# The last layernorm of a four-stage transformer kernel, taken apart: batches normed before the last pair of experts, and that pair's rows summed and written by slot

## The chip, the cores and the metric

The kernel runs on one core of a Trainium2 chip. The metric is the device time of one execution in microseconds (us); lower is better. Five runs of the kernel before give a median of 963.58 us (958.40 to 966.50). The trace that all readings come from is of one more execution, which took 962.57 us; 960.8 us of it lie between the first and the last instruction (the span), at a mean granted TensorE clock of 0.971.

Names: PE is TensorE (PEld its weight loads), DVE is VectorE, ACT is ScalarE, POOL is GpSimd, SP is SyncE, which here only issues DMAs. All data are fp32.

## The reference

The input is x of shape 8 x 512 x 256 (batches, positions, channels). Two layers follow each other, each of an attention part and a feed-forward part, and after each of the four parts `x = layernorm(x + part(x))`. The fourth part is a mixture of experts, and it is the one that the change touches:

```
x = input_emb.reshape(G=2, T=2048, H=256)            # two groups of 4 batches
gate, idx = top_k(softmax(x @ w_router), 2)          # 8 experts, two for each token
# every expert of a group takes at most C=160 slots; later tokens are dropped
expert_in  = einsum('gtec,gth->egch', dispatch, x)
h          = relu(expert_in @ wi[e])                 # 256 -> 1024
expert_out = h @ wo[e]                               # 1024 -> 256
y          = einsum('gtec,egch->gth', combine, expert_out)   # gate * row, added to the token
out        = layernorm(x + y)                        # no scale, no bias
```

A token can be in two experts, in one, or (if both were full) in none.

## The kernel before

**Routing and slots.** The experts are handled in pairs. A pair has 320 slots (160 for each expert), held as three columns of 128, 128 and 64 slots (`COLS`), so that a group has 4 pairs and 12 columns (`NJ`). `route(g)` makes two tables of shape 128 x 12 for a group: `srcs[g]`, the token that sits in each slot, and `gates[g]`, its gate. A slot that stayed empty gets the number of one of 128 spare rows behind the group's 2048 tokens, and gate 0.

**Buffers in HBM.** `x3_d[g]` holds the normed rows of a group, from which the experts read, and `y_d[g]` holds the same rows again as the sum into which the experts' rows are added.

**One expert.** `load_expert` loads `wi` and `wo` (1 MB each) on SP's queue; `EW = 3` experts fit at a time. `gather` fetches the rows of a pair by `srcs` (three indirect DMAs of POOL), `dispatch` transposes them on PE (tile `xs_tp`), `expert_in` is the first matmul (`wi_ps`, with the ReLU on ACT into `e_hT`), `expert_out` the second (`wo_ps`, copied by DVE into `eoT`). `combine` transposes a column back (`eo_tp`) when all its slots are done, scales it by the gates on ACT (`eo`), and adds its rows into `y_d[g]` by an indirect DMA of POOL with `compute_op=add`. Each of these scatter-adds to one `y_d` waits until the one before has landed.

Group 0 goes through experts 0 to 7, group 1 through 7 to 0, so that three experts' weights serve both groups in turn. Step i is the i-th of these 16 (tiles carry this number: `wi_13` is the weights of step 13). The last pair of group 1 is experts 1 and 0, steps 14 and 15.

**The end.** `finish(g)` begins for a group when its last `combine` has ended (key `("s", (g + 1) * E - 1)`): for each batch it loads z, 512 rows of `y_d[g]`, norms it (`layernorm`: statistics on DVE, the power -0.5 on POOL into `ln_rs`, then the scaling, for group 0 on DVE and for group 1 on ACT with a bias `ln_nb` from DVE), and stores it to `out`. For group 0 the four batches follow one another while group 1's experts run; for group 1 all four are loaded at once.

**What sets the order.** Every engine's queue is in fixed order, and that order is planned ahead of time: `interleave` holds a list of streams of stages (keys such as `("h", i)` expert_in, `("e", i)` expert_out, `("s", i)` combine, `("f", g)` finish, `("w", i)` weights, `("r", g)` route), and keeps a model of when engines, PSUM banks and buffers come free (`Plan`, `op`, `pe`, `need`), with costs written out by hand. It always emits the work that the model says can start first. A stage waits for the keys that it names and for free buffers of the tags that it takes. `op` is the helper that emits all planned work of ACT, DVE, POOL and SP, so most of their rows in the profile carry one line, L205; the tile names tell them apart. Where the model sees PE idle for over 1.4 us it puts in `spare` matmuls.

The semaphores' waits come on top of this: an instruction whose data is late holds up all that is queued behind it on its engine.

Of the kernel before, what the change touches and what calls it, by code (L numbers as in the profile page):

```python
# [11 lines left out]
F32 = mybir.dt.float32  # L12
F32R = mybir.dt.float32r
I32 = mybir.dt.int32
# [6 lines left out]
P = 128  # L21
# [6 lines left out]
E = 8  # L28
# [53 lines left out]
def tile_layers(ctx: ExitStack, tc: tile.TileContext, ins, out, at):  # L82
# [41 lines left out]
    def rows_of(d, b):  # L124
        g, r = divmod(b * S, TG)
        return d[g][r : r + S, :].rearrange("(c p) d -> p c d", p=P)
# [39 lines left out]
    def give(tag, t, n=1):  # L166
        Plan.free[tag] += [t] * n
# [67 lines left out]
    def release(ps, t):  # L235
        Plan.banks[Plan.bank_of.pop(id(ps))[1]] = t
# [15 lines left out]
    def later(t):  # L252

        return "other", t

    def interleave(streams):
# [11 lines left out]
        first = {"a1", "b", "c1", "h", "e", "s", "d"}  # L268
# [182 lines left out]
    def route(g, pool):  # L451
# [99 lines left out]
        def sources():  # L551
            nc.vector.tensor_scalar(emp, src, 0.0, float(TG), ALU.is_equal, ALU.mult)
            nc.vector.tensor_scalar(row0, src, 0.0, tokid[:, 0:1], ALU.is_equal, ALU.mult)
            nc.vector.tensor_tensor(emp, emp, row0, ALU.add)
            nc.vector.scalar_tensor_tensor(srcs[g], src, -1.0, emp, ALU.add, ALU.add)
# [9 lines left out]
    with ExitStack() as stages:  # L565
# [15 lines left out]
        def dma(t, out, in_):  # L581
            op(SP, 0.0, t, nc.sync.dma_start, out=out, in_=in_)
# [947 lines left out]

        def combine(i):

            g, e = order[i]
            pair, half = divmod(e, 2)
# [3 lines left out]
            for j, n in enumerate(COLS):  # L1538
# [14 lines left out]
                )  # L1553
                done = op(
# [10 lines left out]
            return done + 2.9  # L1565

        def finish(g):
            for b in range(g * B // G, (g + 1) * B // G):
                z = wk.tile([P, NC, D], F32, tag="x", bufs=XB, name=f"z_{b}")
                t = Plan.t  # L1570
                dma(t, z, rows_of(y_d, b))
                landing = t + (9.0 if g == 0 else 4.0)
                e = max(layernorm(wk, z, z, [landing] * NC, on_act=(g == 1))[3])
                dma(e, out[b].rearrange("(c p) d -> p c d", p=P), z)
                if g == 0:
                    yield later(e + 4.0)
            give("x", e + 4.0, 1 if g == 0 else XB)
            yield later(e + 4.0)
            return e + 4.0

        def after(*keys):
# [62 lines left out]
            ],  # L1644
            [
                (("f", g), [("s", (g + 1) * E - 1)], {"x": 1 if g == 0 else XB}, finish(g))
                for g in range(G)
# [32 lines left out]
```

## Time and profile before

| | |
|---|---|
| median of 5 runs | 963.58 us (958.40 to 966.50) |
| profiled execution | 962.57 us, span 960.8 us |
| busy in the span | PE 894.9 us (93%), DVE 609.2 (63%), ACT 445.4 (46%), POOL 394.5 (41%) |
| last expert matmul (`wo_ps`) | starts 924.30 us, the run of 32 takes 4.51 us |
| last three scatter-adds into `y_d` | issued 925.79, 930.62, 935.13 us |
| loads of group 1's four batches (`z<-y_d`) | issued from 938.73 us on |
| stores of them (`out<-z`) | issued from 948.63 us on, each lands 2.8 us later |

Times within the execution count from the start of the span. A row of the timeline gives start, duration, engine, line, operation, `out<-in` by the program's names (without numbers), shapes, and how long the engine stood idle before it and what ended that. The time of a DMA instruction is that of its issue; it lands later. "Clock" is the share of full speed that the throttle granted TensorE, in the table by stretches of time its mean. "issue" as a releaser means that the profile shows nothing that the engine waited for.

### The profile page before, as it was taken

The numbers are of one execution on the slowest core, as the hardware profiler recorded it, in microseconds if no ns is written. First come the engines' busy times: TensorE is split into PE (matmuls) and PEld (weight loads), VectorE is DVE, ScalarE is ACT, GpSimd is POOL, SyncE is SP. The second block draws the span as 40 slices with busy tenths as digits, with TensorE's granted clock in tenths as the row PEclk, the third lists the DMA queues.
The fourth block names the chain that finished last, engine by engine and source line by source line (L and its number), as shares of the span: only waits on it lengthen the run. The fifth ranks groups of instructions, "written<-read, shape, count | busy, mean of one in ns | idle before, by whom it ended". The sixth has DMA issues, their size and how long they took to land.

```text
span 960.8 us, 18726 instructions
## 1 busy us (share of the span) xinstructions
PE 894.9 (93%) x7676; PEld 702.3 (73%) x7676; DVE 609.2 (63%) x1485; ACT 445.4 (46%) x862; POOL 394.5 (41%) x395
## 2 busy tenths in 40 slices
PE   7999999999999998999999899979999999999960
PEld 4777777777777786778667666657686898999860
DVE  2855446788668678667889788857765853512213
ACT  2237266356834943581656155632655534122213
POOL 3246446432554543372436224362365223253331
PEclk9999999999999999899999899989999999999995
DMA  6030000002000100200020000001503357349735
GB/s 214 2 110 2 2 1 2 2 1 67 1 2 23 45 1 1 67 1 2 1 68 1 1 32 15 2 1 45 190 15 107 130 169 213 67 121 332 215 64 180
DMA packets 49653, 60.36 MB, mean 63 GB/s; under 512 B 5536, under 2 KB 44960, under 8 KB 49568
## 3 DMA queue, kind: packets, MB, share of 16 engines
q1 hardware_dynamic: 45600, 53.92, 16.9%
q0 software_dynamic: 3968, 5.25, 3.2%
q8 instruction: 60, 0.98, 0.4%
q14 instruction: 25, 0.20, 0.1%
HBM read 43.43 MB, written 15.73 MB: 62 GB/s over the span
## 4 chain that ended last, share of the span: by engine, by line
PE 66%; DVE 19%; ACT 6%; POOL 4%; issue 3%; DMA 2%; POOLq 0%; SPq 0%; ACTq 0%; DVEq 0%
PE wi_ps L1484 7%; PE wo_ps L1513 7%; PE pr_ps L1121 6%; PE qk_ps L1201 4%; PE fc_ps L1092 4%; PE qk_ps L876 4%; PE hs L1260 3%; PE w_ps L1354 3%; PE r_ps L957 3%; PE tp L348 3%; PE at_ps L1275 2%; DVE a L205 2%; PE w_ps L1343 2%; PE sc L924 2%; PE v_ps L1207 2%
## 5 line engine op out<-in xcount | busy, mean ns | idle before, releaser
L1121 PE MATMUL pr_ps<-prT,fT 128*128 128x257 f32 x512 | 117.1, 382 | 0.3 <-ACT scm L205 0.3
L1121 PEld LDWEIGHTS pr_ps<-prT,fT 128*128 128x128 f32 x512 | 95.5, 189 | 16.6 <-issue 1.9
L205 POOL TENSOR_TENSOR fsq<-fsq,fsf 128x512 f32<-128x512 f32 x56 | 72.6, 1296 | 30.6 <-ACT fsf L205 28.1
L1484 PE MATMUL wi_ps<-xsT,wi 128*128 128x160 f32 x512 | 77.2, 305 | 0.0
L205 ACT ACTIVATE e_hT<-wi_ps 128x480 f32<-128x480 f32 (+1 forms) x48 | 25.3, 527 | 105.7 <-PE wi_ps L1484 105.7
L1513 PE MATMUL wo_ps<-e_hT,wo 128*128 128x160 f32 x512 | 73.5, 300 | 0.0
L1484 PEld LDWEIGHTS wi_ps<-xsT,wi 128*128 128x128 f32 x512 | 72.5, 194 | 0.7 <-issue 0.2
L1513 PEld LDWEIGHTS wo_ps<-e_hT,wo 128*128 128x128 f32 x512 | 70.5, 190 | 1.0 <-issue 0.6
L205 DVE TENSOR_TENSOR hm<-hs,cst 128x512 f32<-128x512 f32 x96 | 60.0, 676 | 15.5 <-PE hs L1260 15.5
L205 POOL DMA_INDIRECT y_d<-eo,srci x24 | 37.2, 1550 | 77.3 <-ACT eo L205 40.2
L205 POOL TENSOR_TENSOR ln_rs<-ln_rs,mhalf 128x4 f32<-128x4 f32 x32 | 34.1, 1065 | 84.2 <-DVE ln_rs L205 84.2
L205 POOL TENSOR_TENSOR scm<-scm,cst 128x512 f32<-128x512 f32 x32 | 43.8, 1367 | 55.0 <-ACT scm L205 55.0
L205 DVE TENSOR_TENSOR scm<-sc,cst 128x512 f32<-128x512 f32 x96 | 60.1, 677 | 8.9 <-PE sc L924 8.8
L1201 PE MATMUL qk_ps<-l1T,x2T 128*128 128x512 f32 x128 | 61.7, 603 | 0.0
L205 POOL TENSOR_TENSOR hm<-hm,cst 128x512 f32<-128x512 f32 x32 | 40.9, 1280 | 48.2 <-ACT hm L205 48.2
L205 DVE STREAM_TRANSPOSE hT<-pad 128x512 f32<-128x512 f32 x64 | 59.3, 959 | 2.1 <-ACT pad L205 1.4
L876 PE MATMUL qk_ps<-xT,wqkv 128*128 128x512 f32 x128 | 60.2, 613 | 0.2 <-DMA wqkv<-in_L_attn_W_qkv 0.2
L1092 PE MATMUL fc_ps<-x1T_l,fcT 128*128 128x512 f32 x128 | 53.7, 419 | 2.8 <-DVE x1T_l L205 1.5
L1092 PE MATMUL fc_ps<-x1T_h,fcT 128*128 128x512 f32 x128 | 50.8, 397 | 0.0
L205 ACT ACTIVATE x<-x,ln_nb,ln_rs 128x256 f32<-128x256 f32 x64 | 33.2, 590 | 31.2 <-DVE ln_nb L205 31.2
L205 DVE COPY eoT<-wo_ps 128x320 f32<-128x320 f32 x16 | 7.8, 489 | 59.2 <-PE wo_ps L1513 59.2
L205 ACT ACT_TABLE_LOAD x33 | 42.3, 1283 | 1.3 <-PEq L1666 0.7
(240 smaller groups left out, 1997.3 us busy)
## 6 DMA issues: line engine op xcount, KB each, us to landing
wi<-in_L_ffn_wi SPq DMA_DIRECT2D x13, 1024.0 KB, 6.0
wo<-in_L_ffn_wo SPq DMA_DIRECT2D x13, 1024.0 KB, 6.2
x<-in_L_attn_x SPq DMA_DIRECT2D x8, 512.0 KB, 3.9
x_d<-a SPq DMA_DIRECT2D x8, 512.0 KB, 3.0
y_d<-a SPq DMA_DIRECT2D x8, 512.0 KB, 4.1
z<-y_d SPq DMA_DIRECT2D x8, 512.0 KB, 5.1
out<-z SPq DMA_DIRECT2D x8, 512.0 KB, 3.0
prepare<-in_L_ffn_W_fc SPq DMA_DIRECT2D x1, 1024.0 KB, 10.6
```

Source lines behind the costliest of these rows:

```text
L205: heapq.heappush(Plan.events, (t, Plan.count, lambda: fn(*args, **kw)))
L348: T.transpose(ps[:, c * P : (c + 1) * P], src[:, c, k * P : (k + 1) * P], ident)
L876: T.matmul(ps, wqkv[:, k, which * D + m * P : which * D + (m + 1) * P], xT[:, k, :], start=(k == 0), stop=(k == NK - 1),)
L924: T.matmul(sc[p][:, m * 256 : (m + 1) * 256], kT[rows, m, cs], qz[c][rows, m, :, :], start=True, stop=True,)
L957: T.matmul(acc[32 * p : 32 * p + 32, m * P : (m + 1) * P], vz[c][:, m * 4 + p, 32 * j : 32 * j + 32], scm[p][:, m * 2 + j, :], start=False ...
L1092: T.matmul(ps, fcT[:, k, f * P : (f + 1) * P], x[:, k, :], start=(k == 0 and x is low), stop=(k == NK - 1 and x is high),)
L1121: T.matmul(acc[:, : D + 1], hT[:, f, c * P : (c + 1) * P], prT[:, f, :], start=(f == 0), stop=(f == NF - 1),)
L1201: T.matmul(qk, x2T[:, k, cs], l1T[:, k, 0:2, :].rearrange("p a d -> p (a d)"), start=(k == 0), stop=(k == NK - 1),)
L1260: T.matmul(sc[r][:, g * P : (g + 1) * P], hT[rows, g, P : 2 * P], hT[rows, g, :P], start=True, stop=True,)
L1354: T.matmul(acc[:, :D], hT[:, k, c * P : (c + 1) * P], l1T[:, k, 4, :], start=(k == 0), stop=(k == NK - 1),)
L1484: T.matmul(ps[:, f * CAP : (f + 1) * CAP], wi[:, k, (f3 + f) * P : (f3 + f + 1) * P], x[:, k, es], start=(k == 0), stop=(k == NK - 1),)
L1513: T.matmul(ps[:, m * CAP : (m + 1) * CAP], wo[:, f, m * P : (m + 1) * P], hT[:, f, :], start=(f == 0), stop=(f == NF - 1),)
```

## The change

1. Group 1's batches are loaded, normed and stored by a `finish(b)` of their own each, from the end of `combine` of step 13 on: with all experts in them but the last pair (1 and 0).
2. That pair's columns (0, 1, 2) are no longer added into `y_d`. Their scaled rows `eo` stay in SBUF. `meet`, right after the routing, builds `tail_same`: for each of the 320 slots, which of the 320 hold the same token (1.0 or 0.0), from the token numbers spread over all partitions by three matmuls with the identity, and three compares on DVE. `fetch` gathers the 320 slots' rows of `y_d` (as they are after step 13). `sums` multiplies `tail_same` with the rows, so that each slot has the sum of both experts' rows for its token: nine matmuls of 256 columns in three PSUM banks. `finish_last` adds this to the fetched rows, norms them slot by slot, and writes them to their rows of `out` by three indirect DMAs, which wait for all plain stores. Two slots with one token write the same bytes.
3. An empty slot of the last pair now has a token's number (its own partition, 0 to 127) instead of a spare row; with gate 0 it takes part in that token's sum with zeros and writes that token's row.
4. Group 0's batches are finished in two streams side by side ((0, 1) and (2, 3)) instead of one.

The plan is made anew with this. In the planned queues nothing changes place up to the end of group 1's routing. From group 1's second pair on, PE has some `wi_ps` groups ahead of transposes that they followed before; SP has the loads of z_0 and z_2 together, then both stores and the loads of z_1 and z_3 together; the stores of z_1 and z_3 stand ahead of the weights of steps 14 and 15.

```diff
-        first = {"a1", "b", "c1", "h", "e", "s", "d"}
+        first = {"a1", "b", "c1", "h", "e", "s", "d", "z"}
...
             nc.vector.tensor_scalar(row0, src, 0.0, tokid[:, 0:1], ALU.is_equal, ALU.mult)
+            if g == G - 1:
+                nc.vector.memset(emp[:, :3], 0.0)
             nc.vector.tensor_tensor(emp, emp, row0, ALU.add)
...
+        tail, stored = {}, []
         def combine(i):
             g, e = order[i]
+            last = i >= len(order) - 2
...
                     scale=gates[g][:n, col : col + 1], bank=ps, use="scm",
                 )
+                if last:
+                    tail[j], done = eo, t
+                    continue
                 done = op(
                     POOLD, 1.87, max(t, Plan.landed), GP.indirect_dma_start,
                     out=y_d[g], in_=eo[:n], in_offset=None, compute_op=ALU.add,
...
-            return done + 2.9
-        def finish(g):
-            for b in range(g * B // G, (g + 1) * B // G):
-                z = wk.tile([P, NC, D], F32, tag="x", bufs=XB, name=f"z_{b}")
-                t = Plan.t
-                dma(t, z, rows_of(y_d, b))
-                landing = t + (9.0 if g == 0 else 4.0)
-                e = max(layernorm(wk, z, z, [landing] * NC, on_act=(g == 1))[3])
-                dma(e, out[b].rearrange("(c p) d -> p c d", p=P), z)
-                if g == 0:
-                    yield later(e + 4.0)
-            give("x", e + 4.0, 1 if g == 0 else XB)
+            return done + (0.0 if last else 2.9)
+        def meet():
+            g = G - 1
+            token = pools[0].tile([P, 3], F32, tag="tail_token", name="tail_token")
+            row = pools[0].tile([P, 3], I32, tag="tail_row", name="tail_row")
+            def rows():
+                nc.vector.tensor_copy(token, srcs[g][:, :3])
+                nc.vector.tensor_scalar(row, srcs[g][:, :3], g * TG, None, ALU.add)
...
+            for j, n in enumerate(COLS):
+                T.matmul(
+                    ps[:, j * P : j * P + n], token[:, j : j + 1].to_broadcast([P, P]),
+                    ident[:, :n], start=True, stop=True,
+                )
+            same = wk.tile([P, 3, 2 * CAP], F32, tag="T", bufs=TB, name="tail_same")
+            t = pe(0.7)
+            for j in range(3):
+                e = op(
+                    DVE, 0.52, t, V.tensor_scalar,
+                    same[:, j, :], ps[:, : 2 * CAP], token[:, j : j + 1], None, ALU.is_equal,
+                )
...
+        def fetch():
...
+            for j, n in enumerate(COLS):
+                t = op(
+                    POOLD, 1.3, t, GP.indirect_dma_start,
+                    out=y[:n, j, :], out_offset=None, in_=y_d[g],
+                    in_offset=bass.IndirectOffsetOnAxis(ap=srcs[g][:n, j : j + 1], axis=0),
+                )
...
+        def sums(ks, end):
...
+            for j, n in enumerate(COLS):
+                for k in ks:
+                    nk = COLS[k]
+                    T.matmul(
+                        tail["ps"][j][:n, :D], same[:nk, k, j * P : j * P + n], tail[k][:nk],
+                        start=(first and k == ks[0]), stop=(end and k == ks[-1]),
+                    )
...
+        def finish_last():
+            y, (_, row) = tail["y"], tail["same"]
...
+            for j, n in enumerate(COLS):
+                z = y[:n, j, :]
...
+                def stats(z=z, st=st, mv=mv, n=n):
+                    nc.vector.bn_stats(st[:n], z)
+                    nc.vector.bn_aggr(mv[:n], st[:n])
+                    nc.vector.tensor_scalar(st[:n, :1], mv[:n, 1:2], 1.0, LN_EPS, ALU.mult, ALU.add)
+                def put(z=z, j=j, n=n):
+                    nc.gpsimd.memset(between, 0.0)
+                    w = nc.gpsimd.indirect_dma_start(
+                        out=rows, in_=z, in_offset=None,
+                        out_offset=bass.IndirectOffsetOnAxis(ap=row[:n, j : j + 1], axis=0),
+                    )
+                    for store in stored:
+                        tc.add_manual_dep(w.ins, store.ins.name, ...)
+                    for other in written:
+                        tc.declare_no_dep(w.ins, other.ins, reason="the same bytes")
+                    written.append(w)
+                ps = tail["ps"][j]
+                t = op(DVE, 0.45, Plan.t, V.tensor_tensor, z, z, ps[:n, :D], ALU.add, bank=ps)
+                t = op(DVS, 0.8, t, stats)
+                t = op(
+                    POOL, 0.56, t, GP.tensor_tensor, st[:n, :1], st[:n, :1], mhalf[:n], ALU.pow
+                )
+                t = op(
+                    DVS, 0.41, t, V.tensor_scalar,
+                    z, z, mv[:n, 0:1], st[:n, 0:1], ALU.subtract, ALU.mult,
+                )
+                t = op(POOLD, 1.6, max(t, tail["stored"]), put)
...
+        def finish(b):
+            g = b * G // B
+            z = wk.tile([P, NC, D], F32, tag="x", bufs=XB, name=f"z_{b}")
+            t = Plan.t
+            dma(t, z, rows_of(y_d, b))
+            landing = t + (9.0 if g == 0 else 4.0 + 2.9 * (b - B // G))
+            yield later(landing)
+            e = max(layernorm(wk, z, z, [landing] * NC, on_act=(g == 1))[3])
+            def store():
+                stored.append(
+                    nc.sync.dma_start(out=out[b].rearrange("(c p) d -> p c d", p=P), in_=z)
+                )
+            op(SP, 0.0, e, store)
...
+            [(("z", 2), [("z", 1), ("y", 0)], {}, finish_last())],
+            *(
+                [
+                    (("f", b), [("s", (1 + b // half) * E - (1, 3)[b // half])], {"x": 1}, finish(b))
+                    for b in bs
+                ]
+                for bs in ([0, 1], [2, 3], [4], [5], [6], [7])
+            ),
             [
-                (("f", g), [("s", (g + 1) * E - 1)], {"x": 1 if g == 0 else XB}, finish(g))
-                for g in range(G)
+                (("m", 0), [("r", G - 1)], {"T": 1}, meet()),
+                (("y", 0), [("s", n - 3)], {"T": 1}, fetch()),
+                (("z", 0), [("s", n - 2)], {}, sums((2,), False)),
+                (("z", 1), [("s", n - 1)], {}, sums((0, 1), True)),
             ],
```

## Prediction

> **What bounds the kernel now.** I read the page first, then the chain of waits from 880 us on, then windows for clock and DMA, and last POOL's own order.
>
> ```profile
> span 960.8 us, 18726 instructions
> PE 66%; DVE 19%; ACT 6%; POOL 4%; issue 3%; DMA 2%; POOLq 0%; SPq 0%; ACTq 0%; DVEq 0%
> ```
> PE carries the path except at the very end. The chain, cut to the pieces used below (start, duration, what):
>
> ```profile
> 888.53 1.43 POOL y_d L205
> 889.96 1.09 POOL ln_rs L205
> 891.08 1.38 DVE z L205 x4
> 892.46 0.41 DVE eoT L205
> 892.92 0.66 PE eo_tp L1546 x4
> ...
> 924.46 4.36 PE wo_ps L1513 x32
> 928.85 0.50 DVE eoT L205
> ...
> 930.62 3.78 DMA y_d<-eo,srci
> 934.44 0.69 issue
> 935.13 3.58 DMA y_d<-eo,srci
> 938.73 3.92 DMA z<-y_d
> ...
> 954.58 0.60 ACT z L205
> ```
> Two things show. The last expert matmul ends at W = 924.46 + 4.36 = 928.8; after it lie 32.0 us without expert work: two scatter-adds in a row, load of four batches, their layernorm, stores. And at 891 the chain leaves PE: a scatter-add on POOL, the power of one batch's norm queued behind it, the norm on DVE, and behind the norm the copy `eoT` that PE's transposes need. PE stood still from 891.04 to 892.92, 1.9 us. What the stall did to the clock, from the table by stretches (us; PE, PEld, DVE, ACT, POOL busy; granted clock; DMA share; GB/s):
>
> ```profile
> 891.00:894.48 3.48, 1.76 (x12) 1.11 (x10) 1.78 (x5) 1.66 (x4) 0.36 (x2) 1.00 1.02 312
> 894.48:897.89 3.41, 3.41 (x14) 3.40 (x14) 0.00 (x0) 0.93 (x3) 1.28 (x1) 0.50 1.08 343
> ```
> Clock 0.50 for 3.41 us costs another 1.7, so the stall costs 3.6 in all. Why was POOL late? The scatter-add issued at 873.24 landed 8.0 us later, and the next one, to the same rows, waited for it. The DMA queues from 873.3 to 877.3, then from 877.3 to 881.3:
>
> ```profile
> q1 hardware_dynamic: 1406, 1.41, 105.7%
> ```
> ```profile
> q1 hardware_dynamic: 501, 1.21, 79.3%
> q0 software_dynamic: 144, 0.13, 21.2%
> ```
> ```profile
> 881.98 1.56 POOL L205 DMA_INDIRECT y_d<-eo,srci  x1 [7.10 <-issue]
> ```
> While SP's loads with 1 KB rows run, POOL's queue moves no packet; it moves them all once those are through.
>
> **The change, part by part.** Up to 840 us each queue keeps its order, so nothing moves there.
>
> *Token table.* Three fp32 matmuls enter PE where PE is full. A 128x128 pass takes 0.11 (the chain has 0.22 for two of `eo_tp` at 905.11); the trace shows every fp32 matmul as two passes, so two each, the last with 64 columns: +0.55 on the path. The DVE part (a memset and two small copies at about 0.17, three compares at the 0.49 of the `eoT` copy) lies where DVE was idle for 6.8 us; the row gather behind the memset landed 2.5 us before its use. Nothing; without that cover 2 us.
>
> *Group 0 by two batches at a time.* SP now issues z_0 and z_2 together and z_1 and z_3 together, and the stores of z_0 and z_2 stand ahead of z_1's load and of expert 13's weights; DVE has z_2's norm ahead of the copy for expert 10. I followed the planned queues with durations of the trace. PE: wi_11 moves ahead of four `eo_tp` and six `xs_tp` transposes, so these start 4.9 us later, and the scatter-add that was issued at 873.24 goes at about 878.15. Then three 512 KB transfers with 1 KB rows are just ahead of it (store z_2 at 876.5, loads z_1 and z_3): 1.57 MB at the 365 GB/s seen is 4.2, until about 882.6; the one in the trace landed 3.0 after such a drain, so this lands near 885.6. Next issue 0.75 later, 886.35, behind expert 13's second weight load, which drains at 888.2; by the same row (2.2 after the drain) it lands at 890.4, and the third is issued at 891.1. From there as in the chain (888.53 to 892.92 = 4.4): `eo_tp` at 895.5. PE, which now has one wi group more to do first, is ready at 892.7. So the stall stays and grows from 1.9 to 2.8. Bounds: landings free of loads (3.8, as at 915.29 and 919.82) give no stall; the same 15.3 us for the two landings as before gives 5.2. I take 2.8, as the same kinds of transfers stand there. Clock: one slow stretch (1.7) or two (3.4: the 3.03 us stall at 380 us had 6.83 us at 0.50); 2.8 lies between, 2.5. Sum: 2.8 + 2.5 - 3.6 + 0.55 = +2.25, W = 931.05. Queued behind SP's wait for z_1's norm are expert 14's weights: issued at 895.5, landed near 902, used at 908.
>
> Two rules of the Trainium skill, both of which the trace contradicts. "DMA: Bandwidth & Descriptors", section "Queues, rings and completion order", says that an engine takes turns between its queues packet by packet, and its section "Anatomy of one DMA" gives about 2.0 us plus bytes / 436 GB/s, 2.3 for 128 KB; the windows above show no turns and 8.0. By the page there would be no stall, and the sum would be that of the first rival. "TensorE: Matmul & The Clock Gate", section "HAM oscillation", puts the danger at gaps over about 3.4 us; here 1.9 us was enough. By the page the sum would be 2.5 lower.
>
> *Norm of group 1 earlier.* The load of z_4 no longer waits for the last pair's scatter-adds (landed 938.71) but for the pair before it, landed 923.64 = W - 5.2. After, with those scatter-adds 0.1 behind: Z = 931.05 - 5.1 = 925.95; 12.8 us earlier. POOL's three gathers of the last pair's rows (0.96 + 0.3 each) stand before z_4's power but end 2 us before its data: nothing.
>
> *From Z to the last batch's store.* Before: 938.73 to 959.47, 20.74. Added on DVE: the `eoT` copy of the last expert (0.5; now behind z_4's statistics, which wait for the load: data at Z + 3.95, statistics to Z + 6.3, the matmul is done at Z + 5.1, so PE's last transposes start 1.2 us later than they could), and three additions of sums (0.42 each, the row of a 128x256 sum from PSUM) before z_7's bias; these lie in the shadow of its power (1.04 + 0.3). ACT's two copies `eo` (0.83) wait behind z_4's norm and fill its idle time. PE's nine sums of 256 columns, at clock 0.5 about 0.9 each, the last six from about Z + 10.8, end by Z + 16.3, about when DVE asks. Together +0.5 to +1.6, taken as 1.0: Z + 21.75.
>
> *Rows written last.* All stores must land first; then 0.73 from landing to issue (934.40 to 935.13). Two writes in a row, between a gather's cadence (1.27) and a scatter-add's (1.85): 1.55 each. The third tile's power is queued on POOL behind the second write: power 0.8 (1.04 for four columns), norm and hops 0.65, memset 0.1. Write 0 to write 2: 4.65 (4.0 to 5.6). Landing of 64 rows between a gather's 2.44 and a scatter-add's 3.12: 2.65. Sum 8.05. From last landing to the end 1.33, as before.
>
> *Removed:* three scatter-adds from the end; their 8 us are in Z.
>
> **Sum.** 925.95 + 21.75 + 8.05 + 1.33 = 957.1 against 960.8: -3.7. By terms: Z is 12.8 earlier, the rest is 9.05 longer. The profiled execution took 962.57, 1.8 more than its span; the median of five is 1.0 above it, and I forecast medians: 963.6 - 3.7 = 959.9. About 0.5% (4.8 us) is what a measurement here can tell from no change.
>
> **The rivals.**
> 1. *POOL's landings are free, the stall goes.* For: four of the last five of the eight landings listed below took 3.8 or less; had the three transfers drained 2 us sooner, the stall would be under 1. Against: the two windows. No stall: W = 928.8 - 3.6 + 0.55 = 925.75, everything after moves 5.3: 954.6.
> 2. *Slower: the chain of scatter-adds becomes the bound.* Z waits for eight scatter-adds from 878.15 on, each after the last: Z = 878.15 + 8 (t + 0.73). For: with the stall, three of them move beside the weights of experts 14 and 15. Against: the same eight had t = 4.6 on average before (8.0, 5.8, 3.8, 4.9, 3.8, 3.1, 3.8, 3.8), which gives 920.8, 5 us to spare. It decides over t = 5.7 (Z = 929.7, the old end). At 6.4: Z = 935.2, +5.5, 969.1.
> 3. *The writes do not overlap.* If each waits for the landing before it, as scatter-adds do: 2 x (0.73 + 3.8) + 0.73 + 3.1 = 12.9 in place of 8.05: -3.7 + 4.85 = +1.1, 964.7. Against: the code declares them free of each other. Below 1.27 a write could win at most 0.6 on each.
>
> **How the numbers follow.** Forecast 0.48 (its own range 956 to 963: stall 1.3 to 4.3, clock 1.7 to 3.4, tail 1 either way), rival 1 0.30, rival 2 0.12, rival 3 0.10. Range 953.5 to 966.5: it takes in rival 1 with a tail 1 us shorter and leaves out most of rival 2. Over 0.5% faster: rival 1 and some 0.14 of the forecast, 0.44; slower: most of rival 2, a little of rival 3, 0.13; within: 0.43.
>
> **What would show it.** PE waiting 2 to 4 us for `eoT` near 893 and a clock of 0.50 after it; the scatter-add from 878 landing after 7 us; z_4's load about 5 us before the last `wo_ps`; first row write 0.7 after the last store lands, third about 4.7 later; the end 31 us after z_4's load. No stall at 893 means rival 1; a gap over 1 us between the copy `eo` of the pair before the last and its scatter-add means rival 2.

## The result, and the profile after

The changed kernel takes 960.02 us (median of 52 runs, 958.55 to 963.61) against 963.42 us for the kernel before (94 runs, 957.31 to 966.96): a ratio of 0.9974, 95% interval 0.9966 to 0.9982. That is 2.5 us less by the ratio and 3.4 by the medians, and inside the 0.5% that was called no change. The profiled execution took 961.35 us, its span is 959.6 us, and the mean granted clock is 0.975. So the two profiled executions differ by only 1.2 us: the one of before lies 0.85 under the median of its kernel, the one of after 1.33 above.

The stall at 893 us. First its row in the timeline of PE, before and after, then the chain of waits that leads to it.

```profile
892.92 0.66 PE L1546 MATMUL eo_tp<-cst_ident,eoT 128*128 128x128 f32 x4 [1.72 <-DVE eoT L205]
```
```profile
896.31 0.66 PE L1554 MATMUL eo_tp<-cst_ident,eoT 128*128 128x128 f32 x4 [3.17 <-DVE eoT L205]
```
```profile
887.51 1.56 DMA y_d<-eo,srci
889.07 2.65 issue
...
891.93 1.43 POOL y_d L205
893.36 1.09 POOL ln_rs L205
894.44 0.03 issue
894.47 1.38 DVE z L205 x4
895.85 0.41 DVE eoT L205
896.26 0.04 issue
896.31 0.66 PE eo_tp L1554 x4
```
The chain has the same links as before and sits 3.4 us later: scatter-add, power behind it on POOL, norm and copy on DVE, PE. PE waited 3.17 us in place of 1.72. (The prediction's 1.9 counts from 0.16 us earlier, where the chain ends the matmul before; so counted it is 3.3 now.) One stretch at half clock follows (windows; PE, PEld, DVE, ACT, POOL busy; clock; DMA share; GB/s):

```profile
894.77:898.18 3.41, 1.87 (x12) 1.41 (x13) 3.29 (x12) 1.34 (x4) 0.00 (x0) 1.00 0.42 138
898.18:901.59 3.41, 3.41 (x15) 3.41 (x15) 2.00 (x6) 0.24 (x1) 2.60 (x2) 0.50 1.00 289
```
The DMA queues (packets, MB, share of 16 engines) in the four us after the scatter-add of 878.42 was issued, then in the next four:

```profile
q1 hardware_dynamic: 1367, 1.36, 105.0%
```
```profile
q1 hardware_dynamic: 567, 1.32, 87.0%
q0 software_dynamic: 142, 0.13, 20.4%
```
Again POOL's queue moves nothing at first; the scatter-add landed 8.3 us after its issue, 2.8 after the batch load ahead of it.

The tail, from the last scatter-add, in the chain of waits:

```profile
923.08 3.75 DMA y_d<-eo,srci
926.83 0.02 issue
926.85 3.85 DMA z<-y_d
...
946.29 1.10 DMA out<-z
947.39 2.52 issue
949.91 1.05 POOL out L1660
...
951.27 0.98 POOL out L1660
...
952.28 0.58 POOL tail_st L205
...
953.35 1.19 POOLq L1816
```
The load of z_4 starts 4.1 us before the last `wo_ps` ends (930.98). The last plain store lands at 949.08, the row writes follow at 949.91, 951.27 and 953.59, the third behind the power of its tile, and land 2.3 to 2.45 later, the last at 955.90. The span ends at 959.6.

### The profile page after: what moved, and what is told of

Read it like the earlier page. It is cut to its first block, busy times and chain, and to the rows that moved or that the text cites. A ratio compares the mean times of both kernels' runs of the same rounds, so it can differ in the third digit from the quotient of the medians.

```text
span 959.6 us, 18818 instructions
## 1 busy us (share of the span) xinstructions
PE 903.6 (94%) x7704; PEld 707.8 (74%) x7704; DVE 615.2 (64%) x1506; ACT 444.9 (46%) x862; POOL 396.8 (41%) x404
## 5 line engine op out<-in xcount | busy, mean ns | idle before, releaser
L1488 PE MATMUL wi_ps<-xsT,wi 128*128 128x160 f32 x512 | 74.8, 300 | 0.0
L205 POOL DMA_INDIRECT y_d<-eo,srci x21 | 32.5, 1549 | 66.0 <-ACT eo L205 31.1
L294 PE MATMUL spare<-cst,cst_ident 128*128 128x256 f32 x164 | 42.8, 412 | 0.1
```

Source lines behind the costliest of these rows:

```text
L205: heapq.heappush(Plan.events, (t, Plan.count, lambda: fn(*args, **kw)))
L294: T.matmul(ps[:, :256], ident, cst[:, :256], start=True, stop=True)
L1488: T.matmul(ps[:, f * CAP : (f + 1) * CAP], wi[:, k, (f3 + f) * P : (f3 + f + 1) * P], x[:, k, es], start=(k == 0), stop=(k == NK - 1),)
```

## The experiments

Ratios are to the kernel before on the same chip. The three chips of the first eleven gave that kernel medians of 963.0 (first four experiments), 965.5 (next four) and 964.7 us (three more), so times are compared within a chip and ratios across.

**Group 0 in one stream.** The fourth part of the change undone.

```diff
-                for bs in ([0, 1], [2, 3], [4], [5], [6], [7])
+                for bs in ([0, 1, 2, 3], [4], [5], [6], [7])
```


> The changed kernel with group 0's four batches finished in one stream, as before the change; the rest of the change stays. Theory (the two streams put three transfers ahead of one scatter-add and so lengthen PE's stall at 893): the stall is about that of the kernel before, 1.9 us instead of 3.3 in the changed kernel's profile, the last expert matmul 1 to 1.5 us earlier, the time 958.5 to 959 against 960.0. Rival (the stall does not come from the order of group 0's transfers): stall and time stay as in the changed kernel, 960.0 within 0.5.

961.08 us (956.99 to 963.66), ratio 0.9981 (0.9961 to 1.0002). The stall did not shrink; PE's row says

```profile
892.47 1.12 PE L1554 MATMUL eo_tp<-cst_ident,eoT 128*128 128x128 f32 x4 [3.78 <-DVE eoT L205]
```
and 6.83 us at half clock went with it. My theory fell: the stall stands without the two streams too. The time says less than the trace, for the plan made anew differs at the end as well: POOL has the three row writes (943.97 to 948.79) ahead of z_7's power, and z_7's store goes out last (953.15).

**The two streams alone**, in the kernel before.

```diff
+        def finish_early(b):
...
-            [
-                (("f", g), [("s", (g + 1) * E - 1)], {"x": 1 if g == 0 else XB}, finish(g))
-                for g in range(G)
-            ],
+            *(
+                [(("f", b), [("s", E - 1)], {"x": 1}, finish_early(b)) for b in bs]
+                for bs in ([0, 1], [2, 3])
+            ),
+            [(("f", 9), [("s", 2 * E - 1)], {"x": XB}, finish(1))],
```


> The kernel before with nothing but group 0's batches finished in two streams; the end is as it was. Theory: PE's stall at 893 grows from 1.9 to about 3.3 us, and the time by 1 to 2 us, to 964.5 to 965.5. Rival: the stall is not changed by it, 963.4 within 0.5. A gain would say that the two streams are what makes the changed kernel faster.

963.73 us (961.58 to 966.24), ratio 1.001 (0.999 to 1.003), a stall of 3.76 us and 6.83 us at half clock. That is longer than the 1.72 in the trace of the kernel before, but a second trace of that kernel's order (the last experiment) has 4.50, and the times do not separate a cost from no change. So it is not shown that the two streams lengthen the stall.

**Group 0's power on DVE.** The changed kernel, with the link of the chain that sits on POOL moved. The planner is told that nothing changed, so every other queue keeps its order.

```diff
+    def rsqrt_dve(pool, dst, src, scale, eps):
...
-        ready = t = rsqrt(rs, mv[:, :, 1], 1.0, LN_EPS, t)
+        if on_dve:
+            t = op(DVS, 0.17, t, lambda: None)
+            ready = t = op(POOL, power(NC), t, rsqrt_dve, pool, rs, mv[:, :, 1], 1.0, LN_EPS)
+        else:
+            ready = t = rsqrt(rs, mv[:, :, 1], 1.0, LN_EPS, t)
...
-            e = max(layernorm(wk, z, z, [landing] * NC, on_act=(g == 1))[3])
+            e = max(layernorm(wk, z, z, [landing] * NC, on_act=(g == 1), on_dve=(g == 0))[3])
```


> The changed kernel, but the power -0.5 in group 0's norm is worked out by eleven small DVE operations (some 1.8 us for each batch, estimated from 0.16 to 0.17 us rows) instead of one of POOL; the planned order of all else is the same. So the copy that PE needs no longer waits, through DVE's norm, for POOL's scatter-adds. Theory: no stall of PE at 893 and no slow clock after it, the last expert matmul 4.5 to 5 us earlier (926.0 to 926.5 in the profile); the load of batch 4 is then bound by the scatter-adds in a row and comes 4 to 5 us earlier; time 955 to 956. Rival (the scatter-adds in a row are the bound, by rival 2 of the prediction): the stall goes, but the load of batch 4 moves by under 2 us, time 958 to 959.5.

956.39 us (955.34 to 957.68), ratio 0.9929 (0.9902 to 0.9955). The stall and the slow clock behind it are gone, and the last `wo_ps` ends at 923.8 in place of 930.98; 2.1 of these 7.2 us were there before the stall (the `wo_ps` run that began at 885.90 begins at 883.80). So the stall and its slow clock cost 5.1 there. The load of z_4 moved only 3.7, from 926.85 to 923.15, or 1.6 beyond those 2.1. Its chain:

```profile
918.81 0.47 ACT eo L205
919.28 0.08 issue
919.36 3.77 DMA y_d<-eo,srci
923.13 0.02 issue
923.15 3.99 DMA z<-y_d
```
The scatter-adds now decide it, and PE waited for a copy queued on DVE behind z_4's statistics:

```profile
930.03 1.12 PE L1575 MATMUL eo_tp<-cst_ident,eoT 128*128 128x128 f32 x4 [5.21 <-DVE eoT L205]
```

**Rows of 4 KB.** The changed kernel; a batch's loads and stores give each partition four rows in one piece.

```diff
+    def wide_rows_of(d, b):
+        g, r = divmod(b * S, TG)
+        return d[g][r : r + S, :].rearrange("(p c) d -> p c d", p=P)
...
-            dma(t, z, rows_of(y_d, b))
+            dma(t, z, wide_rows_of(y_d, b))
...
-                    nc.sync.dma_start(out=out[b].rearrange("(c p) d -> p c d", p=P), in_=z)
+                    nc.sync.dma_start(out=out[b].rearrange("(p c) d -> p c d", p=P), in_=z)
```


> The changed kernel with the batches of the last stage loaded and stored with four neighbouring rows to a partition, so that these transfers have 4 KB pieces instead of 1 KB; order and bytes are the same. Theory (POOL's queue moves nothing while SP's 1 KB pieces run, but moves along with 4 KB pieces): the scatter-add of 878 lands after about 5 us instead of 8.3; the next one still meets the weights of step 13 in 1 KB pieces and takes 5 to 6; the third is issued about 1.2 earlier, the stall is some 2 us, time 958.5 to 959. Rival (what counts is the sum of bytes ahead): the scatter-add of 878 still takes 7.5 to 8.5 us, stall and time as in the changed kernel within 0.5.

959.99 us (958.38 to 961.78), ratio 0.9959 (0.9942 to 0.9977). The scatter-add issued at 875.30 landed 8.2 us later, and PE waited 3.07. The queues in its first four us (the page's count of packets first), then in the next four:

```profile
DMA packets 427, 1.55 MB, mean 388 GB/s; under 512 B 48, under 2 KB 48, under 8 KB 427
q1 hardware_dynamic: 427, 1.55, 102.4%
```
```profile
q1 hardware_dynamic: 447, 1.28, 83.4%
q0 software_dynamic: 144, 0.13, 20.5%
```
427 packets where there were 1367, and still none of POOL's. So the size of the rows is not the cause. What the traces agree on is the order: POOL's packets move once the transfers issued ahead of them have drained (loads landed at 880.74, the scatter-add at 883.48), whatever their rows.

**The kernel before with group 0's power on DVE.** The same edit as above, in the other kernel.

> The kernel before, and in it one edit: for group 0's four batches the power -0.5 is made by eleven small operations on DVE (a bit trick and three Newton steps) in place of one on POOL; the planned order of PE, ACT and SP stays as it was. My theory: the stall of PE before 893 us is POOL's, the power queued behind a scatter-add that waits for the landing before it; without it the 1.9 us and the 3.4 us at half clock behind it (1.7) go, and nothing else is late, since the last scatter-adds start from the last expert: 963.4 - 3.6 = about 960, as much as the whole change brought. Rival 1: DVE's two extra us a batch delay the copies that PE waits for; then a new stall of 1 to 2 us stands there and the time is 962 to 963. Rival 2: the copy is held by the load of the batch rather than by the power; then the stall stays and so does the time (963 to 964).

958.61 us (956.75 to 961.14), ratio 0.9926 (0.9907 to 0.9945). In the chain PE now goes straight through the place:

```profile
889.08 1.63 PE wi_ps L1505 x12
890.71 0.44 PE eo_tp L1567 x4
891.15 0.99 PE xs_tp L1482 x6
```
The last `wo_ps` ends at 924.73, 4.08 before that of the kernel before; the first scatter-add at 873 was 0.5 early already, so the stall was worth 3.6 in that trace, as the working had it. The times say more, 7 us. The stall does not cost the same in every execution: in a second trace of the kernel before's order (the last experiment) it cost 8.5. The 7 us lie between the two; what it costs on average is not known from two traces. Beside the ratio of the run above, 0.9929, this says the main thing: with the stall cured in both, the rest of the change, as it stands, brings nothing that these intervals can tell.

**Third power first.** The changed kernel, `put` called for the three row tiles after all three are normed.

```diff
-            written = []
+            written, puts = [], []
...
-                t = op(POOLD, 1.6, max(t, tail["stored"]), put)
+                puts.append(put)
+            for put in puts:
+                t = op(POOLD, 1.6, max(t, tail["stored"]), put)
```


> The changed kernel; only one operation of POOL changes place: the power of the third row tile stands ahead of the first of the three row writes in POOL's queue, in place of behind the second. In the changed kernel the writes were issued at 949.91, 951.27 and 953.59 us: 1.36 for the first pair, 2.32 for the second, which had the power (0.58), the norm on DVE (0.41) and the hops between. My theory: the second distance falls to that of the first, 1.36, so that the end comes 1.0 earlier, 959.0. Rival: the third write is held by the queue behind it (descriptors of the second write), not by its norm; then the distance and the time stay (960.0).

962.34 us (959.96 to 963.12), ratio 0.9956 (0.9939 to 0.9973). The interval overlaps that of the changed kernel (0.9966 to 0.9982), so the 1.0 us is not shown by the times; in the timeline of POOL the distances are 1.37 and 1.29, as my theory had it:

```profile
952.73 1.06 POOL L1660 DMA_INDIRECT out<-tail_y,tail_row  x1 [0.75 <-issue]
...
954.10 0.98 POOL L1660 DMA_INDIRECT out<-tail_y,tail_row  x1 [0.19 <-issue]
...
955.39 0.90 POOL L1660 DMA_INDIRECT out<-tail_y,tail_row  x1 [0.19 <-issue]
```

**Plain writes by SP.** They go to the first 320 rows of `out`; the rows of the tokens are left out.

```diff
-                    nc.gpsimd.memset(between, 0.0)
...
-                    w = nc.gpsimd.indirect_dma_start(
-                        out=rows, in_=z, in_offset=None,
-                        out_offset=bass.IndirectOffsetOnAxis(ap=row[:n, j : j + 1], axis=0),
-                    )
+                    w = nc.sync.dma_start(out=rows[j * P : j * P + n, :], in_=z)
...
-                t = op(POOLD, 1.6, max(t, tail["stored"]), put)
+                t = op(SP, 0.0, max(t, tail["stored"]), put)
```


> The changed kernel, but the three row tiles of the last pair are written by three plain DMAs of SP to the first 320 rows of out, not by POOL's indirect DMAs to the rows of their tokens; they still wait for all four stores. In the changed kernel the third row write landed at 955.90 us and the execution's last instruction ended at 959.6, 3.7 later, with a DRAIN of POOL from 953.35 to 958.78 among the last; in the kernel before, whose last indirect DMA was issued at 935.13, the end came 1.33 after the last landing. My theory: POOL's drain at the end of the program waits some 4.3 us behind its last indirect DMA, and that is 2.4 us of the changed kernel's end. Then here the writes follow the last store at SP's own pace, land about 2.5 to 3 us after it (952), and the end comes 1.3 later: a span of about 953.3, a time of 953.5 to 954.5. Rival: the 3.7 us are something every engine has to do after a late DMA, whoever issues it; then the end is 3.7 after the last landing, a span of about 955.7 and a time of 956.

957.86 us (954.33 to 959.04), ratio 0.9915 (0.9898 to 0.9931). The three writes go out 0.4 apart from 947.83 on, the last lands at 950.68, and the span ends at 952.6, 1.9 after that landing, between the two theories. POOL's DRAIN (an instruction at the end of its queue) was again long, though no DMA of POOL was near: it ended at 951.76, 4.0 after POOL's last power. So my theory had the right row and the wrong cause; the last experiment asks again.

**An earlier chain.** Group 0 in one stream with its power on DVE and a planned landing of 7 in place of 9 us, the third power first, the sums free of the row fetch, the row tiles planned behind the last store. Of the edit, what the runs above do not have:

```diff
-            landing = t + (9.0 if g == 0 else 4.0 + 2.9 * (b - B // G))
+            landing = t + (7.0 if g == 0 else 4.0 + 2.9 * (b - B // G))
...
-            [(("z", 2), [("z", 1), ("y", 0)], {}, finish_last())],
+            [(("l", 0), [("z", 1), ("y", 0), ("f", 7)], {}, finish_last())],
...
-                for bs in ([0, 1], [2, 3], [4], [5], [6], [7])
+                for bs in ([0, 1, 2, 3], [4], [5], [6], [7])
...
-                (("z", 0), [("s", n - 2)], {}, sums((2,), False)),
+            ],
+            [
+                (("z", 0), [("s", n - 2), ("m", 0)], {}, sums((2,), False)),
```


> A version put together from what was seen so far: the changed kernel with group 0's batches in one stream (planned landing 7 in place of 9 us) and their power on DVE, the third row tile's power ahead of the row writes, the first three sums planned free of the row fetch (they now stand ahead of the last wo_ps), and the row tiles planned after the last store. The chain of eight scatter-adds starts as in the kernel before, some 5 us earlier than in the changed kernel. With group 0's power on DVE alone (956.4) the load of z_4 came at 923.15 us with the last wo_ps ending at 924.3, that is, the chain of scatter-adds set it. My theory: with the chain 5 us earlier that load goes near 918 and everything behind it 4 to 5 us earlier, less what the last expert's rows then need: 951 to 952.5, minus 1 for the third power: 950 to 951.5. Rival 1: the last rows' sums become the bound (last wo_ps near 924, sums near 932, norms to 936), which leaves 2 us of the 5: 953. Rival 2: z_3's finish now lies just ahead of z_4's load on SP's queue and holds it; then the load comes at 923 again and the time is 955 to 956.

956.36 us (955.12 to 959.11), ratio 0.9904 (0.9884 to 0.9924): faster than either kernel, but some 3 us short of what I expected (950 to 951.5, from times of the first chip; the ratio gives 953.8 there). The chain of scatter-adds began at 874.73, only 1.6 before that of the run with the power on DVE alone, and z_4's load came at 922.34. The last `wo_ps` ended at 929.0 in place of 923.8: three sums stood ahead of it (1.6), and PE waited 1.2 for a copy behind the statistics of a batch whose load took 10.0 us. Another wait of 1.2 stood at 849. What one end won the other lost.

**The bias later.** The changed kernel, `ln_nb` planned half a us later and the landing of each of group 1's last three batches 6.5 us after its load (in place of 6.9, 9.8 and 12.7). In the trace DVE's order differs by the place of three `ln_nb` alone, each one statistic later; ACT has its last two copies `eo` ahead of z_4's scaling instead of behind it.

```diff
-                DVS, 0.16, t, V.scalar_tensor_tensor, nb, ...
+                DVS, 0.16, t + (0.5 if on_act == 2 else 0.0), V.scalar_tensor_tensor, nb, ...
...
-            landing = t + (9.0 if g == 0 else 4.0 + 2.9 * (b - B // G))
+            landing = t + (9.0 if g == 0 else (4.0 if b == B // G else 6.5))
```


> The changed kernel with one thing moved in the tail: the bias of each batch of group 1 (ln_nb on DVE, which waits for POOL's power) is planned behind two of the next batch's four statistics, as in the kernel before, and not behind one. In the changed kernel the stores were issued at 936.67, 939.83, 943.06 and 946.29 us, 3.2 apart; in the kernel before 2.6 to 2.7 apart. My theory: the term 'from the load to the last store', predicted at 21.75 and measured at 22.23 against 20.74 before, is longer because DVE stands idle before each bias (the power takes 1.02, one statistic fills 0.5 of it); it is not longer because of the added copies and sums. Then the last three stores come 0.5 closer each and the end 1.5 earlier: a time 1.5 below the changed kernel's, a ratio to the kernel before of about 0.996. Rival: ACT (2.1 us for one batch's scaling, and the two copies eo between) or the row tiles' sums set the distance; then the stores stay 3.2 apart and the ratio stays at 0.9974.

959.63 us (958.00 to 962.94), ratio 0.9953 (0.9933 to 0.9973). The rows of `ln_nb` on DVE in the changed kernel (idle time before them at the end), then here:

```profile
937.53 0.16 DVE L205 SCALAR_TENSOR_TENSOR ln_nb<-ln_mv,ln_rs 128x4 f32<-128x4 f32 x1 [0.64 <-POOL ln_rs L205]
940.76 0.16 DVE L205 SCALAR_TENSOR_TENSOR ln_nb<-ln_mv,ln_rs 128x4 f32<-128x4 f32 x1 [0.64 <-POOL ln_rs L205]
```
```profile
937.61 0.16 DVE L205 SCALAR_TENSOR_TENSOR ln_nb<-ln_mv,ln_rs 128x4 f32<-128x4 f32 x1
940.32 0.17 DVE L205 SCALAR_TENSOR_TENSOR ln_nb<-ln_mv,ln_rs 128x4 f32<-128x4 f32 x1
```
The idle time is gone, the stores are 2.5 to 2.7 apart, and the last one lands 20.84 after z_4's load (22.23 in the changed kernel, 20.74 before). So that part of the tail was lost to the position of one small instruction. The times alone do not show it: the intervals of the two ratios overlap.

**All that helped**, in the changed kernel's PE order: power on DVE, third power first, and one planned landing for group 1's batches, which puts `ln_nb` behind two statistics and the last copy `eoT` ahead of z_4's.

```diff
-            landing = t + (9.0 if g == 0 else 4.0 + 2.9 * (b - B // G))
+            landing = t + (9.0 if g == 0 else 6.0)
```


> All that was seen to help, in the order of the changed kernel: group 0's power on DVE (956.4 alone), the third row tile's power ahead of the row writes (second distance between writes 2.3 to 1.3), the bias behind two statistics, and DVE's last copy eoT ahead of z_4's statistics (with the power on DVE alone, PE waited 5.2 us for that copy). PE's order is that of the changed kernel. My theory: 956.4 - 1.0 - 1.5 = 953.9 on the same footing, a ratio of 0.990 (0.988 to 0.992); the load of z_4 stays near 923, set by the chain of scatter-adds. Rival: the last store no longer decides and the row tiles come last (their sums wait for the last expert); then only 1.0 of the 2.5 is left, 955.4, ratio 0.992.

955.22 us (955.02 to 955.58), ratio 0.9898 (0.9880 to 0.9917), as expected, and the lowest ratio of the kernels that do all the work (the earlier chain's 0.9904 is not told apart from it). z_4's load came at 923.63. Against the kernel before with the same cure (0.9926) that is 0.3% or some 2.7 us: what the change is worth once its own tail is repaired, by ratios whose intervals still touch.

**Without group 0's norm.**

```diff
-                for bs in ([0, 1], [2, 3], [4], [5], [6], [7])
+                for bs in ([4], [5], [6], [7])
```


> The same, but group 0's four batches are neither loaded, normed nor stored (their final layernorm is left out), so that beside the chain of eight scatter-adds only the weights move. It asks what keeps the load of z_4 at 923 once the stall is cured. My theory: each scatter-add's packets wait until the transfers issued ahead of them have drained; with 4 MB less of those the eight landings fall from 5.0 us on average to about 4.2, and the load of z_4 comes at 916 to 918, 5 to 7 earlier. The end then comes only 2 to 3 earlier, since the last expert still ends near 924 and its copy eoT stands ahead of the batches' statistics on DVE: a span of about 951. Rival: the weights alone make the landings long; then the load stays within 2 us of 923 and the end within 1.

954.59 us (951.85 to 956.40), ratio 0.9895 (0.9870 to 0.9919); against the version above the load of z_4 came 4.2 earlier (919.45) and the span ended 2.6 earlier (951.2), nearer to my theory than to the rival; the medians differ by 0.6 only, within their noise. But the plan put the first scatter-add at 872.69, 4.6 earlier, and from there to z_4's load it was 46.8 us, as above (46.3). The first two landings were short (at most 4.1 and 4.7), but the third, fourth, sixth and seventh scatter-add then waited for their rows: ACT's copies `eo` ended at 882.7, 891.6, 902.0 and 910.8, and they went out 0.3 to 0.6 later. So the chain did not get shorter; where the landings do not bound it, its rows do, and how much of the eight landings is group 0's traffic stays open.

**One late instruction of POOL**, in the kernel before.

```diff
+            if g == 1:
+                last = pools[0].tile([P, 1], F32, tag="last_pool", name="last_pool")
+                op(POOL, 0.2, e, GP.tensor_tensor, last, z[:, NC - 1, :1], mhalf, ALU.mult)
```


> The kernel before with one operation more: when ACT has scaled the last batch (z_7, 956.7 us in the kernel before), POOL multiplies one of its columns into a spare tile that nothing reads. In the kernel before POOL's last instruction, the power for z_7, ended at 954.35 and POOL's DRAIN at the end of the program ended at 958.35, 4.0 later and ahead of the last landing (959.47); the last instruction of the execution came 1.33 after that landing. With the row tiles written plainly, POOL's last instruction ended at 947.75 and its DRAIN at 951.76, again 4.0 later, though no DMA of POOL was near; in the changed kernel it was 4.25 after the third row write. My theory now: the DRAIN takes 4.0 us after POOL's last instruction, whatever that is, and the end comes 0.83 after it or 1.33 after the last landing, whichever is later. Then here the DRAIN ends near 961 and the execution's last instruction comes about 2.2 after the last landing. Rival, my theory of the plain writes: the DRAIN is long only behind POOL's DMAs; then the end stays 1.33 after the last landing.

One run, on a fourth chip: 965.73 us beside 959.90 for the kernel before, a difference that one run does not carry; the reading is inside the trace. POOL's added instruction:

```profile
958.96 0.19 POOL L205 TENSOR_TENSOR last_pool<-z,mhalf 128x1 f32<-128x1 f32 x1 [2.38 <-ACT z L205]
```
From the sequencers' rows of the traces (us; the last landing of this run is its issue, 958.91, and the 2.8 that stores take):

| kernel | POOL's last instruction ends | POOL's DRAIN ends | last landing | span ends |
|---|---|---|---|---|
| before | 954.35 (power) | 958.35 | 959.47 | 960.8 |
| changed | 954.53 (row write) | 958.78 | 955.90 | 959.6 |
| plain writes | 947.75 (power) | 951.76 | 950.68 | 952.6 |
| one late instruction | 959.15 (product) | 963.16 | 961.7 | 964.0 |

The DRAIN ends 4.0 us after POOL's last instruction (4.25 where that is a DMA), and the span ends 0.8 after the DRAIN. Only in the kernel before was there something later, a store. The rival is out.

This trace answers a second question. Up to the added instruction each queue holds what it holds in the kernel before, in the same order, so it is a second trace of the stall at 893 without the change. PE's row, and the windows' line for the slow stretch:

```profile
892.84 1.11 PE L1546 MATMUL eo_tp<-cst_ident,eoT 128*128 128x128 f32 x4 [4.50 <-DVE eoT L205]
```
```profile
890.74:900.98 10.24, 8.14 (x30) 7.24 (x31) 1.78 (x5) 2.19 (x5) 3.38 (x3) 0.50 0.73 196
```
4.50 us in place of 1.72, and 10.24 at half clock in place of 3.41. PE came to the place 2.86 us earlier (its `wi_ps` run at 886.55, before at 889.41), but the scatter-add in front of the power went out at 888.46, before at 888.53; behind the stall PE was 2.03 late (`wo_ps` at 901.00, before at 898.97). So the stall cost 4.9 more than in the first trace, 8.5 in place of 3.6. Reckoned in the same way against the traces with the power on DVE, it cost 5.1, 5.0, 6.6, 7.0 and 5.5 in the five traces with the changed kernel's order there (the changed kernel, rows of 4 KB, third power first, plain writes, bias later).

## Why the prediction was right, step by step

The forecast of the time, 959.9, was met (960.0), and its main reading in the main: the stall stays, and what the earlier load wins is mostly given back. That the stall grows is not shown: with the changed kernel's order it cost 5.0 to 7.0 us in five traces, with the order of before 3.6 and 8.5 in two. The load of z_4 came 11.9 us earlier and the span from there to its end grew by 10.7. But the terms were not all right, and part of the agreement is chance: the sum asked for a span 3.7 shorter, the profiled span was 1.2 shorter.

| step | predicted | profile after |
|---|---|---|
| token table | +0.55 | +0.6 (a `wi_ps` run at 849.74 moved to 850.59, 0.2 of it there since before 640 us) |
| first scatter-add, issue and landing | 878.15, 885.6 | 878.42, 886.75 |
| stall | 2.8 | 3.17 (3.3 by the count of the prediction) |
| lost to the clock | 2.5 | 1.7 |
| end of the last `wo_ps` (W) | 931.05 | 930.98 |
| load of z_4 (Z) | 925.95 | 926.85 |
| from Z to the last store's landing | 21.75 | 22.23 |
| from there to the third row write's landing | 8.05 | 6.82 |
| from there to the end | 1.33 | 3.70 |

- *The stall.* Its size was right and its account half right. "While SP's loads with 1 KB rows run, POOL's queue moves no packet" is true of these rows, but the rows' size has no part in it (the run with 4 KB rows). The three transfers named as ahead of the scatter-add were the right ones. "Group 0 by two batches at a time" as the cause of a growth is not shown: in one stream the stall is as long, and with the order of before it was once longer. Its "the windows above show no turns" holds for the first window of each pair; in the second both queues move.
- *Clock.* One stretch, not between one and two. The stall came out 0.5 longer and the clock 0.8 cheaper, so W was met because two errors nearly cancel. In two of the other traces with this order it was two stretches.
- *Z.* 0.9 late: the rows (`eo`) of the next to last scatter-add were ready at 917.32, and it went out at 918.55, 1.2 later, since the one before had landed at 917.83. That is the second rival's mechanism at its edge, and its sign (a gap over 1 us) was there. The bound that the prediction gave it, t = 5.7, is where the old time would be reached; by its own formula the chain passes the forecast Z at t = 5.25 (878.15 + 8 x 5.98 = 926.0). With the stall cured it takes over.
- *From Z to the last store.* +1.5 where I had taken +1.0, and for another reason: not the added copies and sums, but `ln_nb` behind one statistic. I had compared which instructions are added, not where the old ones stood between the new.
- *Row writes.* 1.2 too dear: 1.36 from the first to the second write, where I had 1.55, and 0.58 for the third tile's power, where I had 0.8; the landing took 2.31, not 2.65. The third rival is out: the writes overlap.
- *The end.* The step that failed: "From last landing to the end 1.33, as before." In the kernel before that row was short because POOL had been done for 5 us; here POOL writes last, and its DRAIN stands 2.9 us beyond the landing: 2.4 us not in the sum. The DRAIN was in the trace of before too, hidden behind a store.
- *Removed scatter-adds.* Worth less than their 8 us in two ways: Z cannot come before the eight that are left, and the tail behind Z is longer than the one it replaces.

Rival 1 (no stall) was the wrong account of the change and the right account of what was to be had: its 954.6 is close to the 956.4 of the run that removes the stall, and the 955.2 of the best one.

## What to carry to other kernels

Before work is moved out of a tail, look for a small step that sits on the wrong queue: here one power behind a scatter-add that waits for a landing held up an engine that was not waiting for either, and moving that power alone brought the old kernel to the ratio that the new one has with it (0.9926 and 0.9929). Before a wait is called longer or shorter by a change, look at it in more than one trace of the same order: here it cost 3.6 us in one and 8.5 in another. Where an engine becomes the last to work, cost what its queue does after its last instruction; a row that is short in the profile before may be short only because something else covers it. And a change that makes the plan anew also moves small instructions that it does not name, such as the bias here: compare their neighbours, not only the counts.

## What the runs showed of the hardware that I had not expected

- POOL's DRAIN at the end of the program ends 4.0 us after its last instruction, a product of one column included.
- The order of DMA queues. POOL's packets waited for transfers issued ahead on SP's queue to drain with rows of 1 KB and of 4 KB alike, and then moved along with the later ones (142 packets beside 567). Not all of that time is the loads': on free queues the first packet of a scatter-add moves 2.1 us after its issue (919.82 to 921.92 in the kernel before), in the changed kernel that of 878.42 moved 5.1 after (883.53). The Trainium skill's "DMA: Bandwidth & Descriptors", "Queues, rings and completion order", lets an engine take turns between queues packet by packet; that fits the second window of each pair and not the first.
- The clock's stretches begin and end on a grid of 3.41 us: in the changed kernel those at half clock begin at 382.77, 529.54, 631.94 and 898.18, 43, 30 and 78 times 3.413 apart. So the same wait costs more or less by where it falls. PE waits 3.0 us at 380 us in every traced execution. The window behind it in the changed kernel, then the one in the run with the power on DVE:

```profile
382.80:386.20 3.40, 2.52 (x10) 2.43 (x11) 2.52 (x7) 1.12 (x2) 0.70 (x1) 0.50 0.00 0
```
```profile
384.60:388.00 3.40, 3.40 (x46) 2.58 (x45) 2.45 (x10) 2.97 (x4) 0.81 (x2) 1.00 0.00 0
```
  In the first, 6.83 us passed at half clock, in the other none; PE then ran some 3 us ahead, some of which is lost again at the wait that begins at 629 us. The kernels do the same there. So two single profiles may differ by 3 us in a stretch that no edit touches, and are compared from a mark behind it. The Trainium skill's "TensorE: Matmul & The Clock Gate", "Part 1: The HAM clock gate", has such a free-running window of about 3.4 us, which agrees.
